# A graph layer on one core: shared scratch for the layer norm, earlier first counts, and h split in four parts

## The chip, the cores and the metric

The kernel runs on one core of one Trainium2 chip, and uses its five engines: TensorE (PE; its weight loads are shown as PEld), VectorE (DVE), ScalarE (ACT), GpSimd (POOL) and SyncE (SP, which only issues transfers). The metric is device time in microseconds (us). A run's time is that of the whole execution; the profile's span is the part in which the program's instructions were recorded.

## The reference

One layer of a graph network with a layer norm ahead of it, over 6,250 nodes with 64 features and 206,250 edges (100,000 random pairs in both directions, and one loop at each node), sorted by target:

```python
h = jnp.maximum(_layernorm(x, axis=-1), 0.0)
msg = h[src] + edge_attr_64
agg = segment_sum(msg, dst, num_segments=6250)
x = x + relu(agg @ W1 + b1) @ W2 + b2
```

The layer norm needs a mean and a variance for each node, and the sums over edges need for each node a sum of rows of h and a sum of edge features.

## The kernel before, in words

**Most of the sum over h goes without a gather.** The first 178 groups of 1,024 edges are put into 1,862 tiles, each of up to 128 edges with targets in V = 3 neighbouring nodes. For a tile, DVE makes 0/1 codes of the edges' sources ("hot", function rows_of_tiles, L832, 18 tiles at a time, from the digits made by encode, L813 and L819, 36 tiles at a time). PE multiplies them to a 128 x 147 table of counts, six tiles to a step (function count, L846, tile pc), and ACT copies the counts into a ring (L852). A block is 84 tiles, 14 steps; there are 22 blocks and 311 steps. While block b is counted, block b - 1 is multiplied with h: 49 products of 128 x 252 accumulate in pv (function products, L864), spread over steps 1 to 8 of the block. For that h is kept as an upper and a lower half side by side (h2; split_upper L547 and L548, split_lower L553). Block 0 has no products beside it.

**The words.** The edges' sources and targets are packed into one word each in DRAM (L579 to L582). To find a tile's words the kernel searches where its first edge lies: a coarse search by DVE and PE, one row of 256 targets per tile fetched by POOL (fetch_row, L283, 15 gathers for 15 groups of 128 tiles), a count by ACT (seek, L298, an activation with an accumulator), and a short sum by DVE (place, L303 and L305). Then POOL gathers the words (fetch_pair), DVE unpacks two groups of tiles at a time (unpack_pair, L655 to L674), and PE and ACT turn them (turn, L688 to L699, with an Exp at L699).

**Edge features.** The features of the edges of these first nodes are loaded in 132 chunks of 1,536 edges straight from DRAM by SP (L405), turned into sums by PE (chunk_sum, L429, with DVE's chunk_hot, L418) into the tile bank, copied out by ACT (take_sums, L437), and placed in pv by PE (chunk_place, L459). The first node of a chunk is found by chunk_starts, chunk_rows, chunk_columns and chunk_index (L324 to L354); fetch_dst gathers the targets, chunk_nodes (L367, L368) and chunk_turn (L375, L376) lay them out.

**The last 24 groups** are gathered: POOL adds rows of h from a table in DRAM to the loaded features, one gather for 128 edges (pfeat, L283, 188 gathers), and PE sums two groups at a time at one of two steps in a block (features_h, L482 to L489, step 5 or 11). The table is written by norm_h (L537 and three transfers at L538); table_rows (L621 to L623) makes the gather's indices.

**"Seconds".** Tiles that have more than 128 edges get a second tile: second_flags, second_ranks and second_words (L721 to L762) find them; each goes from DVE to PE and back to DVE. POOL then gathers their words, they are unpacked over four steps, and turned.

**The order of work is written out by hand.** Every engine runs its instructions in the order of the program. Ahead of step 0 stands a head: loads, searches, packing, mean, centring with squares on ACT, variance, root, scale, table, and the first unpack. Then the loop over steps calls, at each step n, what a dictionary `before` holds for n, then count(n), rows_of_tiles at n % 3 == 1 (for the three steps from n + 2 on), products, and lists of later work. DVE's tiles for three steps are double-buffered, and so is pc. POOL's gathers are issued from a queue by a planner: a clock of HEAD_US for a step of block 0 and STEP_US = 1.4 for a later one, GATHER_US = 2.0 for a gather; features_h of a pair of groups is put at the first step 5 or 11 of a block at which the planner's clock is 4 us past the end of the pair's gathers.

**Scratch.** In the kernel before, the head's scratch (squares, rows of targets, mean, variance, root, and the upper halves) lies in the array of sums, which holds the result of all blocks. So the sums are set to zero late, by ACT in four parts at steps 11 to 14 (L557), and every block's products are added (L895).

## Time and profile before

| what | value |
| --- | --- |
| median of three runs | 504.35 us (502.35 to 505.71) |
| the profiled execution's own time | 503.97 us |
| its span | 502.3 us |
| PE, PEld busy | 429.1 us (85%), 374.7 us (75%) |
| DVE, ACT, POOL busy | 354.3 us (71%), 351.8 us (70%), 374.1 us (74%) |
| mean granted TensorE clock | 0.943 |
| chain that ended last | PE 53%, ACT 14%, DVE 11%, POOL 10%, issue 6%, DMA 5% |

The profile is of one execution. A row of the timeline has the start, the time until the end of the last of the instructions that it merges, the engine, the line, the operation, the tiles written and read, the count, and in brackets the idle time of the engine before it with what ended it. A row of groups has the busy time, the mean in ns, and the idle time before the group. A row of windows has, for a stretch, the busy time and number of instructions of PE, PEld, DVE, ACT and POOL, the granted clock, the share of the DMA engines, and GB/s.

### The profile page before, as it was taken

How to read it: one execution, taken by the hardware profiler on the slowest of the kernel's cores; microseconds unless marked ns; L12 is line 12 of the kernel's file. 1: busy time of each engine (PE TensorE's matmuls, PEld its weight loads, DVE VectorE, ACT ScalarE, POOL GpSimd, SP SyncE). 2: the span in 40 equal slices, each digit the busy share in tenths (PEclk: the TensorE clock that was granted, in tenths of full speed). 3: DMA queues.
4: the chain of work that ended last, by engine and by line, in shares of the span. 5: the costliest groups of instructions: out<-in, count | busy, mean ns of one | idle time of the engine just before them, and what ended most of it. 6: DMA issues, size and time to landing. Idle time of an engine off the chain costs nothing.

```text
span 502.3 us, 17233 instructions
## 1 busy us (share of the span) xinstructions
PE 429.1 (85%) x7194; PEld 374.7 (75%) x7195; DVE 354.3 (71%) x776; ACT 351.8 (70%) x517; POOL 374.1 (74%) x260
## 2 busy tenths in 40 slices
PE   3023799998879998999999999999998999999984
PEld 3023688877768788888788888888887888888864
DVE  4799858977588765787758757787666686677721
ACT  3628978687556767768688778778776677677650
POOL 6866848888887788888888888888888888885000
PEclk9556779999989998999999999999998999999998
DMA  8849637587465665857658758659658568567310
GB/s 225 238 130 301 142 72 190 135 198 174 115 154 127 170 148 133 191 139 187 162 119 211 170 127 217 156 122 246 149 134 216 102 148 204 129 154 168 107 38 15
DMA packets 113355, 78.65 MB, mean 157 GB/s; under 512 B 32736, under 2 KB 108632, under 8 KB 113048
## 3 DMA queue, kind: packets, MB, share of 16 engines
q1 hardware_dynamic: 84356, 65.87, 45.0%
q0 software_dynamic: 28624, 10.11, 17.1%
q10 hardware_dynamic: 292, 1.52, 0.9%
q8 instruction: 58, 0.95, 0.8%
q14 instruction: 25, 0.20, 0.1%
HBM read 73.48 MB, written 3.99 MB: 154 GB/s over the span
## 4 chain that ended last, share of the span: by engine, by line
PE 53%; ACT 14%; DVE 11%; POOL 10%; issue 6%; DMA 5%; DVEq 0%; POOLq 0%; ACTq 0%
PE pv L864 20%; PE pc L846 17%; POOL pfeat L283 9%; ACT ring L852 8%; PE bank L429 6%; DMA pfeat<-table,src_p 4%; DVE hot L832 2%; PE bank L486 2%; PE po L942 2%; ACT kq L695 2%; PE pv L459 2%; PE ph L934 1%; ACT kv L699 1%; DMA firsts_i<-in_dst_g 1%; PE pk L688 1%
## 5 line engine op out<-in xcount | busy, mean ns | idle before, releaser
L283 POOL DMA_INDIRECT pfeat<-table,src_p x188 | 325.9, 1734 | 60.7 <-issue 51.5
L852 ACT ACTIVATE ring<-pc 128x882 fp32r<-128x882 f32 x310 | 276.7, 924 | 82.1 <-PE pc L846 70.4
L846 PE MATMUL pc<-hot 128*128 128x147 fp8e4 x1862 | 178.4, 234 | 25.2 <-ACT ring L852 13.5
L832 DVE TENSOR_TENSOR hot<-at,of 128x576 int32<-128x576 bf16 x208 | 163.2, 826 | 41.4 <-PE pc L846 30.6
L864 PE MATMUL pv<-ring,h 128*128 128x252 f32 (+1 forms) x1078 | 171.3, 296 | 0.8 <-ACT ring L856 0.8
L846 PEld LDWEIGHTS <-hot 128*128 128x128 fp8e4 x1862 | 128.7, 101 | 49.4 <-issue 21.8
L864 PEld LDWEIGHTS pv<-ring,h 128*128 128x128 f32 x1078 | 140.5, 192 | 1.2 <-ACT ring L856 1.0
L429 PE MATMUL bank<-feat,hotf 128*18 128x64 f32 x3168 | 73.5, 225 | 3.1 <-issue 2.0
L429 PEld LDWEIGHTS bank<-feat,hotf 128*18 128x18 f32 x3168 | 49.2, 99 | 21.6 <-issue 4.8
L895 DVE TENSOR_TENSOR sums<-sums,pv 128x252 f32<-128x252 f32 (+4 forms) x34 | 10.0, 323 | 52.8 <-PE pv L864 37.6
L418 DVE TENSOR_TENSOR hotf<-rel,iota 128x432 f32<-128x432 bf16 (+1 forms) x67 | 39.8, 595 | 0.0
L695 ACT ACTIVATE kq<-pk 128x512 bf16<-128x512 f32 (+18 forms) x48 | 18.4, 449 | 12.8 <-PE pk L688 10.2
L813 DVE TENSOR_TENSOR at<-iota_a,kq 128x576 bf16<-128x576 bf16 (+1 forms) x52 | 23.5, 452 | 0.5
L936 ACT ACTIVATE after<-ph,b1s 128x252 f32<-128x252 f32 (+3 forms) x26 | 12.0, 469 | 15.3 <-PE ph L934 14.0
L283 POOL DMA_INDIRECT sums<-in_dst_g,row_i x15 | 17.4, 1162 | 7.0 <-issue 4.3
L819 DVE TENSOR_TENSOR of<-of,kv 128x432 bf16<-128x432 bf16 (+1 forms) x52 | 20.0, 385 | 3.3 <-DVE of L813 0.5
L283 POOL DMA_INDIRECT words<-packed,first_i x15 | 17.7, 1181 | 4.6 <-issue 4.0
L947 DVE TENSOR_TENSOR after<-po,after 126x128 f32<-126x128 f32 (+3 forms) x26 | 7.5, 288 | 18.1 <-PE po L942 18.1
L934 PE MATMUL ph<-sums,w1s 128*128 128x252 f32 (+3 forms) x52 | 17.1, 417 | 3.1 <-issue 1.8
L813 DVE TENSOR_TENSOR of<-iota_w,kq 128x432 bf16<-128x432 bf16 (+1 forms) x52 | 19.5, 374 | 0.0
L324 PE MATMUL pstart<-begins,first 128*1 128x9 f32 (+2 forms) x30 | 1.6, 172 | 17.2 <-DVE sums L509 9.3
L942 PE MATMUL po<-w2s,after 128*126 128x64 f32 (+3 forms) x104 | 15.9, 278 | 0.2 <-issue 0.2
(183 smaller groups left out, 315.6 us busy)
## 6 DMA issues: line engine op xcount, KB each, us to landing
feat<-in_edge SPq DMA_DIRECT2D x132, 384.0 KB
pfeat<-in_edge SPq DMA_DIRECT2D x23, 256.0 KB
pfeat<-table,src_p POOLq DMA_INDIRECT x188
out_y<-after SPq DMA_DIRECT2D x23, 63.0 KB
dstn<-in_dst_g SPq DMA_DIRECT2D x1, 1024.0 KB
table<-xl SPq DMA_DIRECT2D x2, 512.0 KB
after<-in_x SPq DMA_DIRECT2D x4, 252.0 KB
packed<-dstn ACTq DMA_DIRECT2D x1, 768.0 KB
```

The source lines that it names most:

```text
L283: nc.gpsimd.indirect_dma_start(out=rows, out_offset=None, in_=source, in_offset=bass.IndirectOffsetOnAxis(ap=index, axis=0), compute_op=op)
L418: nc.vector.tensor_tensor(hot_of[u][:, :n].rearrange("p c j w -> p (c j) w"), rel[:, c:c + n].rearrange("p c q k -> p (c q k)").unsqueeze( ...
L429: nc.tensor.matmul(bank[q * QP:q * QP + WQ, at:at + D], hot_of[u][:, c, j, :], feats[u][c][:, j, :], start=(k == 0), stop=(k == JP - 1))
L695: nc.scalar.activation(kq[:, q, at:at + n].rearrange("s i k o -> s (i k) o"), pk[:, q, a:a + n].rearrange("s i k -> s (i k)").unsqueeze(2) ...
L813: nc.vector.tensor_tensor(to[:, :n].rearrange("s i k (m o) -> s (i k) m o", o=2), iota_k.rearrange("s (m o) -> s m o", o=2).unsqueeze(1).t ...
L819: nc.vector.tensor_tensor(pairs_of, pairs_of, kv[:, c:c + n].rearrange("s i k o -> s (i k) o").unsqueeze(2) .to_broadcast([P, 2 * n, WE // ...
L832: nc.vector.tensor_tensor(hot[:, :n, c:c + m * A8].rearrange("s i (w a) -> s i w a", a=A8), at[:, o:o + n, k].unsqueeze(2).to_broadcast([P ...
L846: nc.tensor.matmul(pc[:, k, q * K:(q + 1) * K], hot[:, i, :P], hot[:, i, P:P + K], start=True, stop=True)
L852: nc.scalar.activation(to.rearrange("p h (k m) -> p h k m", k=2), pc[:, :, :ST // 2 * K].rearrange("p k (m h) -> p h k m", h=HI), AF.Copy)
L864: nc.tensor.matmul(pvs[b], h2[:, h, :], ring[:, h, c:c + columns_of_block(b)], start=(h == 0), stop=(h == HI - 1))
L934: nc.tensor.matmul(ph[:, :n], w1s, agg[:, start[b]:start[b + 1]], start=True, stop=True)
L942: nc.tensor.matmul(po[:pairs[b], k, :], hid[:, k:2 * pairs[b]:2], w2s, start=True, stop=True)
```

## The change

It makes these edits; the rest of the kernel is as before.

- **Scratch.** A tile "scratch" takes the place of the head's use of the array of sums. It shares its memory with h2, which is made later. Nine rows of targets (ROWS) are kept instead of eleven and four, and row i lies in slot i % 9.
- **Clears.** The sums are cleared in the head: POOL 2,000 columns ahead of its first gather, ACT 1,000 ahead of L562, DVE 2,000 ahead of the packing and the rest (390) behind it. Columns of blocks 0 to 3 (966) are not cleared, and add_products copies into them. ACT's four clears at steps 11 to 14 go.
- **Root.** Square root and reciprocal become Ln and an Exp with scale -0.5, both on ACT; the Newton step on DVE stays. ACT's first activation is an Exp instead of a Sqrt, and an Ln on a column of ones stands behind turn(0).
- **Order of the head.** place covers groups 3 to 6 at once behind the centring; chunk_starts, chunk_rows, chunk_columns and the first unpack follow, then the variance. rows_of_tiles(0) stands ahead of the last third of the variance and of the root. POOL fetches row 0 to 8, words 0 and 1, rows 9 and 10, the targets of chunk group 0 (behind chunk_index), rows 11 to 14, words 2 and 3. ACT seeks rows 9 and 10 ahead of turn(0), and rows 11 to 14 behind it, ahead of the root and of the first ring copy.
- **Into the steps.** norm_scale and the three norm_h with their transfers go to steps 2, 3 and 4, table_rows to step 5, place(7, 4) to step 3 and place(11, 4) to step 5; fetch_h starts at step 5 instead of 2.
- **Split of h.** In four parts (12, 12, 12 and 13 of 49) instead of three, at steps 11 to 18 instead of 7 to 10; the upper halves go through the first 768 or 832 columns of the sums, one after another.
- **Later work.** second_flags, second_ranks, find_groups and second_words go from steps 13, 15, 12, 17 to 18, 20, 21, 22; the unpack of the seconds from 21 to 24 to 26 to 29, and their turn from 25 to 30. take_sums(0) goes from step 14 to 19 and the first chunk_place from 16 to 20.
- **Planner.** HEAD_US is 1.45 instead of 1.7, and POOL's clock opens at step 5 instead of 3.

The core of the diff:

```diff
-HEAD_US = 1.7
+HEAD_US = 1.45
...
-    h2 = consts.tile([P, HI, 2 * D], F32R, name="h2")
+    scratch = consts.tile([P, HI * 2 * D], F32, tag="h2", name="scratch")
...
-    nc.scalar.activation(root, zero, AF.Sqrt)
+    nc.scalar.activation(root, zero, AF.Exp)
...
+    def clear(engine, n):
+        a, z = cleared[0], min(cleared[0] + n, ACOLS)
+        cleared[0] = z
+        if engine is nc.scalar:
+            nc.scalar.activation(agg[:, a:z], zero.to_broadcast([P, z - a]), AF.Copy)
+        else:
+            engine.memset(agg[:, a:z], 0.0)
...
     def norm_root():
         nc.vector.tensor_scalar(var, var, 1.0 / D, EPS, op0=OP.mult, op1=OP.add)
-        nc.scalar.activation(t, var, AF.Sqrt)
+        nc.scalar.activation(tmp, var, AF.Ln)
+        nc.scalar.activation(rs, tmp, AF.Exp, scale=-0.5)
...
+    fourths = [(0, 12), (12, 24), (24, 36), (36, HI)]
...
-            nc.vector.tensor_tensor(to, to, pv[:, c:c + z - a], op=OP.add)
+            if b <= SB:
+                nc.vector.tensor_copy(to, pv[:, c:c + z - a])
+            else:
+                nc.vector.tensor_tensor(to, to, pv[:, c:c + z - a], op=OP.add)
...
-    for i in range(11, IC):
+    for i in range(ROWS, ROWS + 2):
         fetch_row(i)
-    place(6, 3)
+    place(3, 4)
     chunk_starts(0, 2 * RC, "pc", 2)
-    src_hi = late.tile([P, GP * J], I32, tag="part", name="src_hi")
-    table_rows(src_p, src_hi)
-    for f in unpack_pair(0):
-        f()
     chunk_rows(0, 2 * RC)
     load(0)
     chunk_columns(0, 2, "pc", 2)
-    turn(0, P, columns(0))
-    seek(9, 3)
-    norm_scale()
+    nc.vector.tensor_copy(identb, ident)
+    for f in unpack_pair(0):
+        f()
     chunk_index(0, 2)
     fetch_dst(0)
+    for i in range(ROWS + 2, IC):
+        fetch_row(i)
     fetch_pair(2)
-    for k in range(3):
-        norm_h(k)
+    seek(ROWS, 2)
+    turn(0, P, columns(0))
+    nc.scalar.activation(root, ones[:, :1], AF.Ln)
+    seek(ROWS + 2, IC - ROWS - 2)
+    norm_var(0)
+    norm_var(1)
+    rows_of_tiles(0)
+    norm_var(2)
+    norm_root()
     load(1)
...
-        1: [lambda: seek(12, 3), lambda: chunk_nodes(0)],
-        2: [lambda: [fetch_h(g) for g in range(GA, GA + 4)], lambda: chunk_turn(0)],
-        3: [lambda: place(9, 3)],
-        5: [lambda: place(12, 3)],
-        7: [lambda: split_upper(0), lambda: split_upper(1)],
-        8: [lambda: split_lower(0), lambda: split_lower(1)],
-        9: [lambda: split_upper(2)],
-        10: [lambda: split_lower(2)],
-        12: [find_groups],
-        13: [second_flags],
-        15: [second_ranks],
-        17: [second_words],
+        1: [lambda: chunk_nodes(0)],
+        2: [lambda: chunk_turn(0), norm_scale, lambda: norm_h(0)],
+        3: [lambda: norm_h(1), lambda: place(7, 4)],
+        4: [lambda: norm_h(2)],
+        5: [lambda: table_rows(src_p, src_hi), lambda: place(11, 4),
+            lambda: [fetch_h(g) for g in range(GA, GA + 4)]],
+        11: [lambda: split_upper(0)],
+        12: [lambda: split_lower(0)],
...
+        17: [lambda: split_upper(3)],
+        18: [lambda: split_lower(3), second_flags],
+        20: [second_ranks],
+        21: [find_groups],
+        22: [second_words],
...
-    for k in range(4):
-        before.setdefault(11 + k, []).append(lambda k=k: clear(k, 4))
...
-    n = 25
+    n = 30
...
-            at_step(n + STEPS, take_sums, b)
+            at_step(n + STEPS + (0 if b else 5), take_sums, b)
             for u in of_block[b]:
-                at_step(n + STEPS + 2, chunk_place, u)
+                at_step(n + STEPS + (2 if b else 6), chunk_place, u)
...
-            if n == 3:
+            if n == 5:
                 pool[0] = clock(n - 1) + OPENING_US
```

More of the change, by code (lines that the diff above doesn't have):

```diff
@@ L290, in fetch_row @@
     def fetch_row(i):
[L291 to L292 removed]
+        at = rows_at + i % ROWS * L1
+        rows_of[i] = scratch[:, at:at + L1].bitcast(I32)
         gather(rows_of[i], dst_g.rearrange("q h (r k) -> (q h r) k", k=L1), row_i[:, i:i + 1])
@@ L498, in gnn_kernel @@
     xh = xl
-    stat = agg[:, stat_at:stat_at + 4 * HI].rearrange("p (k h) -> p k h", k=4)
-    mean, var, rs, t = (stat[:, k, :] for k in range(4))
+    stat = scratch[:, stat_at:stat_at + 4 * HI].rearrange("p (k h) -> p k h", k=4)
+    mean, var, rs, tmp = (stat[:, k, :] for k in range(4))
     thirds = [(0, 16), (16, 32), (32, HI)]
@@ L514, in norm_center @@
         nc.vector.tensor_tensor(xh[:, h0:h1], xh[:, h0:h1], wide(mean, h0, h1), op=OP.subtract)
-        part = agg[:, squares_at + h0 * D:squares_at + h1 * D].rearrange("p (h d) -> p h d", d=D)
+        part = scratch[:, squares_at + h0 * D:squares_at + h1 * D].rearrange("p (h d) -> p h d", d=D)
         nc.scalar.activation(part, xh[:, h0:h1], AF.Square)
@@ L551, in split_lower @@
     def split_lower(k):
-        h0, h1 = thirds[k]
+        h0, h1 = fourths[k]
         nc.vector.tensor_tensor(h2[:, h0:h1, D:], xh[:, h0:h1], uppers.pop(k), op=OP.subtract)
-    def clear(k, n):
-        a, z = ACOLS * k // n, ACOLS * (k + 1) // n
-        nc.scalar.activation(agg[:, a:z], zero.to_broadcast([P, z - a]), AF.Copy)
-    for i in range(6):
+    clear(nc.gpsimd, 2000)
+    for i in range(ROWS):
         fetch_row(i)
     srcf = src.bitcast(F32)
+    clear(nc.scalar, 1000)
     nc.scalar.activation(srcf, src, AF.Copy)
@@ L586, in gnn_kernel @@
     place(0, 3)
-    for i in range(6, 11):
-        fetch_row(i)
     for k in range(3):
```

43 lines of the change are left out of this document (23 added, 20 removed).

## The prediction

> **What bounds the kernel now.** I read the page's busy shares first, then the stretches of the time, then each stretch's own groups and waits. The stretches: the head from the first full pass over x to the first count, the steps to the seconds, the rest of block 1, and all that follows.
>
> ```profile
> 17.85:42.83 24.98, 3.60 (x26) 2.79 (x27) 23.99 (x52) 12.09 (x30) 17.26 (x14) 0.50 0.64 203
> 42.83:69.90 27.07, 20.56 (x284) 17.62 (x284) 22.07 (x46) 25.80 (x38) 18.20 (x10) 0.70 0.69 170
> 69.90:88.00 18.10, 17.80 (x358) 15.73 (x356) 13.92 (x37) 12.88 (x19) 13.33 (x7) 1.00 0.52 134
> 88.00:480.00 392.00, 367.99 (x6343) 322.29 (x6342) 283.01 (x609) 288.12 (x415) 313.23 (x187) 0.99 0.66 158
> ```
>
> The columns are the stretch, its length, and busy us of PE, PEld, DVE, ACT, POOL, then granted clock, DMA share, GB/s. In the first row DVE works 23.99 of 24.98 us: the head is DVE's. From 69.90 PE works 17.80 of 18.10, and 94% from 88 to 480: what comes early to 69.9 comes early to the end, unless POOL's gathers hold PE. In the second row ACT has 25.80 of 27.07 and DVE 22.07; DVE's missing 5 us are these waits for PE, and the tiles for step 18 (L832, end 69.78) stand behind the first two:
>
> ```profile
> DVE flag L728 <- PE pnext L726: 2.3, 1, 2.3
> DVE fl L744 <- PE prk L736: 1.9, 1, 1.9
> ```
>
> ```profile
> 68.20 1.58 DVE L832 TENSOR_TENSOR hot<-at,of 128x576 int32<-128x576 bf16 x2
> 72.28 0.15 DVE L759 CAST second_i<-pxn 14x1 int32<-14x1 f32 x1 [2.51 <-PE pxn L757]
> ```
>
> So DVE sets the pace from 17.85 to 69.78, with 2.3 + 1.9 us of waiting. A change that only reorders DVE's work can win those 4.2 us, the instructions that it drops or puts behind step 18, and lose the waits that it makes. That is the sum I work out. DVE's prices, by groups from 17 to 70 us (busy us, mean ns, idle):
>
> ```profile
> L832 DVE TENSOR_TENSOR hot<-at,of 128x576 int32<-128x576 bf16 (+1 forms) x14 | 11.0, 827 | 0.3
> L553 DVE TENSOR_TENSOR h<-xl,sums 128x1024 fp32r<-128x1024 f32 (+1 forms) x3 | 3.6, 1239 | 0.0
> L514 DVE TENSOR_TENSOR xl<-xl,sums 128x1024 f32<-128x1024 f32 (+1 forms) x3 | 3.6, 1239 | 0.0
> L537 DVE SCALAR_TENSOR_TENSOR xl<-xl,sums 128x1024 f32<-128x1024 f32 (+1 forms) x3 | 3.6, 1239 | 0.0
> L521 DVE TENSOR_REDUCE sums<-sums 128x16 f32<-128x1024 f32 (+1 forms) x3 | 3.5, 1235 | 0.0
> L509 DVE TENSOR_REDUCE sums<-xl 128x49 f32<-128x3136 f32 x1 | 3.4, 3423 | 2.2 <-issue 2.2
> L547 DVE TENSOR_SCALAR sums<-xl 128x1024 int32<-128x1024 int32 (+1 forms) x3 | 2.0, 701 | 0.0
> L813 DVE TENSOR_TENSOR at<-iota_a,kq 128x576 bf16<-128x576 bf16 x4 | 1.8, 452 | 0.0
> L418 DVE TENSOR_TENSOR hotf<-rel,iota 128x432 f32<-128x432 bf16 x3 | 1.8, 600 | 0.0
> L819 DVE TENSOR_TENSOR of<-of,kv 128x432 bf16<-128x432 bf16 x4 | 1.5, 384 | 0.3
> L813 DVE TENSOR_TENSOR of<-iota_w,kq 128x432 bf16<-128x432 bf16 x4 | 1.5, 377 | 0.0
> ```
>
> A set of tiles (two of L832) is 1.6 us, an encode (L813 twice, L819) 1.2, a chunk_hot (L418) 0.6.
>
> **The change, part by part.** *Clears.* DVE waits 2.2 us ahead of L509, which keeps its place, and I cost the four clears at nothing: DVE's larger one has the wait for the packing in front of it, the small one those 2.2 us; POOL's and ACT's stand ahead of waits for DVE and the loads. Without that cover POOL's would delay the first row by its own length, at most about 2 us. ACT loses four clears from a stretch that it fills; but with the split spread out, DVE and not ACT then sets those steps.
>
> *First counts.* They no longer stand behind norm_h (3.6), the scale (five instructions, about 1.4), the last third of the variance (1.2) and table_rows (0.9): 7.1 us earlier. They get two waits. POOL's rows:
>
> ```profile
> 21.77 1.94 POOL L283 DMA_INDIRECT sums<-in_dst_g,row_i  x1 [0.30 <-issue]
> 24.02 2.03 POOL L283 DMA_INDIRECT sums<-in_dst_g,row_i  x1 [0.30 <-issue]
> ...
> 27.60 0.94 POOL L283 DMA_INDIRECT words<-packed,first_i  x1 [0.30 <-issue]
> ...
> 36.68 1.81 POOL L283 DMA_INDIRECT dstq<-in_dst_g,cols_i  x1 [3.13 <-DVE cols L354]
> ...
> 45.74 1.70 POOL L283 DMA_INDIRECT pfeat<-table,src_p  x1 [3.67 <-DMA table<-xl]
> ```
>
> ```profile
> 30.49 0.29 DVE L655 TENSOR_SCALAR code<-words 128x256 int16<-128x256 int16 x1
> ...
> 34.59 0.44 DVE L529 RECIPROCAL sums<-sums 128x49 f32<-128x49 f32 x1
> ```
>
> The words take the places of the gathers at 21.77 and 24.02, so they are issued by 26.05. Before, those issued by 28.54 were there by 30.49, so landing takes at most 1.95, and I take 28.0. DVE is through centring and chunk starts at about 26.5 (17.85 + 3.4 + 0.2 + 3.6, place, a wait of 0.35 for PE's pstart, chunk rows 0.8): it waits 1.5 us for words. Then unpacking, two thirds of the variance, encode and tiles (3.5 + 0.3 + 2.3 + 1.2 + 1.6) end at 36.9: the first count comes some 5.5 us earlier than 42.83.
>
> *Root.* On DVE the reciprocal (0.44) goes. On ACT root and first ring copy now stand behind the seeks of rows 11 to 14, whose gathers stand on POOL behind the targets' gather, which waits for chunk_index at 31.8. Five gathers with 0.30 between them, by 0.94 each, are issued by 38.0; by 2.03 each, by 43.5. The rows at 21.77 and 24.02 ran beside L514, a DVE operation with two operands, those of 0.94 mostly beside operations with one; the new ones run beside the variance and then encode and tiles. I take two slow ones, 40; landing 1.9 and a seek more, the root is there at about 42.0 (39.9 to 45.5). DVE has finished chunk_nodes and the second set of tiles by 40.9 and waits 1.1 us (0 to 4.6). ACT's table:
>
> ```profile
> 38.54 1.28 ACT L699 ACT_TABLE_LOAD   x1
> ```
>
> This load leaves the path, with the first Exp placed at the start; a new one for Ln fits into ACT's wait for rows. Ln and Exp themselves I price as the root that they replace, twice. The Trainium skill (ScalarE: Activation LUTs, section on table sets) says that one set holds both exp and ln; by that rule nothing stands between the two. Were they in two sets, the load of 1.28 us in the row would come between them and the root 1.3 us later; no run shown so far settles it.
>
> *Norm in the steps.* It is moved work on DVE, not new: scale, three norm_h, table_rows now stand ahead of the tiles for steps 6 and 9, so these come no earlier than before. SP's table transfers follow norm_h at about 46.7 instead of 40; ahead of them on SP are only loads with free buffers. POOL's first gather of the table, 5.7 us behind norm_h before, comes at 52.4 instead of 45.74. Behind it:
>
> ```profile
> POOL words L283 <- DVE second_n L761: 6.0, 1, 6.0
> ```
>
> Those 6.0 us of POOL's waiting shrink to about 1, since second_n, at step 22, finds POOL's queue less far ahead. So the gathers fall some 1.5 us behind the old ones.
>
> ```profile
> 120.36 1.80 POOL L283 DMA_INDIRECT pfeat<-table,src_p  x1 [0.30 <-issue]
> ```
>
> ```profile
> 130.84 1.13 PE L486 MATMUL bank<-after,pfeat 128*64 128x42 f32 x32
> ```
>
> That gather is the last of the second pair of groups; it ends at 122.16, PE uses it at 130.84, at step 61, which keeps its place: 8.7 us, less 1.5, less the landing. Covered. By the planner's constants seven other pairs move by 6 or 8 steps later (33 to 39 up to 299 to 305), the last still ahead of the tail: same work, no price.
>
> *Split.* Four parts cost DVE what three did, 3 x (0.70 + 1.24) = 5.8, but the last, 1.45, now stands behind the tiles for step 18. One scratch for all uppers makes each upper wait for ACT's copy of the one before; with the double buffer of tiles I take 1.1 us of such waits (0 to 2).
>
> *Ledger at the tiles of step 18:* 69.78, less 4.2 (waits), 0.44 (reciprocal), 1.3 (the short instructions of groups, flags and ranks, my estimate), 1.45 (last part), plus 1.5, 0.35, 1.1, 1.1 (waits made) = 66.3. The last part of the split and the flags with PE's pnext (1.45 + 1.3) follow ahead of the count of step 18: 69.1.
>
> ```profile
> 70.65 0.83 PE pxn L755 x30
> 71.48 0.76 PE pxn L757 x30
> ...
> 73.49 0.40 PE pc L846 x6
> ```
>
> Before, that count came at 73.49: a lead of 4.4 us.
>
> *Seconds.* Of PE's work that stood ahead of it, pxn (0.83 + 0.76), the ranks' prk and the first chunk_place (about 0.55 each) now follow: 2.7 us back. And at step 22 DVE waits for pxn and then has an encode, a set of tiles and a chunk_hot to make (1.2 + 1.6 + 0.6), while PE has two counts and some six products, about 1.7: a stall of 0 to 2. I take 1.0. The lead left is 0.7 us, between 4.5 ahead (no wait for the root, none for the split, no stall) and 5 behind (root at 45.5, all waits full).
>
> **The sum.** 503.97, the profiled execution's own time, less 0.7: 503.3 us. That execution lies 0.4 under the median of three. About 1% is what a measurement of this kernel can tell from no change.
>
> **The rivals.** *The lead of the first count is kept.* If the waits for words and root are short and the seconds fall into gaps, 5.5 us arrive at the end: 498.5. For it speaks PE's 17.80 of 18.10 behind step 16, against it DVE's full head: tiles past the second set wait for moved work.
>
> *Seconds in the loaded steps make it slower.* Before, DVE waited 2.3, 1.9 and 2.5 us for PE in three round trips, two of them while PE had little to do. Now each stands in block 1's products. If each also stops PE for its length, 6.7 us are lost against a lead of 1.7: 503.97 - 1.7 + 6.7 = 509.0. It decides against the change from 1.7 us of stalls on, and by over 1% from 6.7. Against it: DVE makes tiles three steps ahead, 3 to 4 us of PE's work.
>
> *The words land no sooner.* Then the unpack starts at 30.49 again, 2.5 us later than I take: 505.8. For it: the rows show the packed words stored by 26.35, not yet by 21.8; against it, their store on ACT stands behind L579, which ends 2.2 us ahead of L509.
>
> *POOL is locked out by DVE.* All five gathers by 2.03: the root 3.5 us later, 506.8. The Trainium skill (SBUF — State Buffer, section on who interferes with whom) says that a DVE instruction with two SBUF inputs contends with a GpSimd instruction that reads SBUF, while a reduction doesn't; by that rule the encode and tiles would hold the later rows' gathers. The rows of 1.94 and 2.03 against 0.94 agree.
>
> **How the numbers follow.** My forecast has 0.46; words late 0.09 and POOL locked 0.11, which both lie within 1% of before; the kept lead 0.2, the slower seconds 0.14. Faster by over 1%: 0.2; within 1%: 0.66; slower: 0.14. The likeliest case's own range is 499.5 to 506. For 8 in 10 I take in the kept lead and leave out most of the slowest: 498.5 to 507.5.
>
> **What would show it.** The first count (L846) near 37, ACT's first ring copy near 42, with rows 11 to 14 as its releaser; DVE idle ahead of L655 and ahead of the scale; tiles for step 18 near 66; POOL's first pfeat near 52 with a shorter wait for second_n; PE idle at steps 22 to 24. The prediction is wrong if the ring copies start before 40, if PE shows no gap behind pxn, or if L486 at step 61 waits for a gather.

## The result, and the profile after

The changed kernel took 509.25 us in the median of four executions (507.89 to 512.88), the kernel before 503.35 (500.67 to 505.71): ratio 1.015, 95% interval 1.0102 to 1.0198. The forecast was 503.3 with a range up to 507.5. The rival of the seconds in the loaded steps had said 509.0. The profiled execution took 507.89 us, with a span of 506.2. Ratios and intervals here and below are taken from fast executions (none over 1.5% above the fastest of its kernel), medians from all, so a ratio need not be that of the medians (here 1.012).

The stretches of the profile after, cut at the same work as before (to the first count, to the seconds, to step 30, and the 392 us that follow), with the same columns:

```profile
17.80:37.34 19.54, 3.63 (x27) 2.55 (x27) 16.57 (x37) 11.57 (x28) 12.84 (x11) 0.50 0.80 252
37.34:69.83 32.49, 19.99 (x277) 16.50 (x277) 27.68 (x52) 23.64 (x40) 18.52 (x12) 0.75 0.53 145
69.83:91.90 22.07, 20.00 (x358) 17.79 (x358) 13.54 (x40) 11.92 (x16) 13.72 (x9) 0.85 0.45 108
91.90:483.90 392.00, 366.72 (x6346) 321.23 (x6346) 283.97 (x614) 288.87 (x417) 311.12 (x188) 0.99 0.66 159
```

The head is 5.4 us shorter, the steps behind it 5.4 longer. The loss stands in the third row: 22.07 us instead of 18.10, with PE busy for 20.00 instead of 17.80 on the same 358 matmuls. PE's work became slower there: the granted clock is 0.85 and was 1.00.

The head first, by three engines' instructions in order of time (start, length, then in brackets the idle time ahead and its releaser). DVE:

```profile
28.80 0.29 DVE L661 TENSOR_SCALAR code<-words 128x256 int16<-128x256 int16 x1 [2.14 <-DMA words<-packed,first_i]
...
34.70 0.38 DVE L819 TENSOR_TENSOR of<-iota_w,kq 128x432 bf16<-128x432 bf16 x1
...
35.70 1.58 DVE L838 TENSOR_TENSOR hot<-at,of 128x576 int32<-128x576 bf16 x2
...
42.77 0.21 DVE L542 TENSOR_TENSOR scratch<-scratch 128x49 f32<-128x49 f32 x1 [1.52 <-ACT scratch L538]
...
66.55 1.57 DVE L838 TENSOR_TENSOR hot<-at,of 128x576 int32<-128x576 bf16 x2
68.04 0.58 DVE L560 TENSOR_SCALAR sums<-xl 128x832 int32<-128x832 int32 x1
68.66 1.02 DVE L566 TENSOR_TENSOR h<-xl,sums 128x832 fp32r<-128x832 f32 x1
69.61 0.17 DVE L729 TENSOR_SCALAR ends<-first 128x15 f32<-128x15 f32 x1
```

ACT, around the root:

```profile
38.33 0.51 ACT L310 ACTIVATE scratch<-scratch,nhalf 128x256 bf16<-128x256 int32 x1 [1.57 <-DMA scratch<-in_dst_g,row_i]
...
40.96 0.23 ACT L537 ACTIVATE scratch<-scratch 128x49 f32<-128x49 f32 x1
41.20 1.28 ACT L538 ACT_TABLE_LOAD   x1
42.49 0.24 ACT L538 ACTIVATE scratch<-scratch 128x49 f32<-128x49 f32 x1
```

POOL, the gathers of rows 11 to 14, the first of the table, and the one behind second_n:

```profile
33.39 0.95 POOL L295 DMA_INDIRECT scratch<-in_dst_g,row_i  x1 [0.30 <-issue]
34.64 0.95 POOL L295 DMA_INDIRECT scratch<-in_dst_g,row_i  x1 [0.30 <-issue]
35.89 1.38 POOL L295 DMA_INDIRECT scratch<-in_dst_g,row_i  x1 [0.30 <-issue]
37.58 0.95 POOL L295 DMA_INDIRECT scratch<-in_dst_g,row_i  x1 [0.30 <-issue]
...
51.94 2.17 POOL L295 DMA_INDIRECT pfeat<-table,src_p  x1 [10.69 <-DVE first_i L317]
...
80.78 1.28 POOL L295 DMA_INDIRECT words<-packed,second_i  x1 [6.22 <-DVE second_n L767]
```

The head went much as forecast: the words at 28.80, the root's chain at 42.77, tiles for step 18 done at 68.12, the first gather of the table at 51.94. Step 18 came 3.0 us earlier than before. PE's first count, and then what it met from step 18 on:

```profile
37.34 1.66 PE L852 MATMUL pc<-hot 128*128 128x147 fp8e4 x12 [4.44 <-DVE hot L838]
...
69.83 0.40 PE L731 MATMUL pnext<-ends,shift 128*128 128x15 f32 x2 [2.27 <-DVE ends L729]
...
70.65 1.73 PE L870 MATMUL pv<-ring,h 128*128 128x252 f32 x7
...
77.29 1.07 PE L870 MATMUL pv<-ring,h 128*128 128x252 f32 x7
...
83.89 0.53 PE L441 MATMUL bank<-feat,hotf 128*18 128x64 f32 x24 [1.95 <-DVE hotf L430]
...
97.60 0.58 PE L387 MATMUL pdst<-shift,dstq 128*128 128x128 f32 x3 [2.31 <-DVE dstq L380]
```

Three times PE waits about 2 us for DVE. Behind the first wait seven products take 1.73 us; a few steps on, seven take 1.07. The same place cut into stretches, the three waits and what follows each:

```profile
67.50:69.83 2.33, 0.07 (x1) 0.00 (x0) 2.25 (x5) 1.17 (x2) 2.02 (x2) 1.00 0.32 27
69.83:74.38 4.55, 4.54 (x30) 4.42 (x31) 2.41 (x7) 2.65 (x4) 3.94 (x3) 0.62 0.25 54
74.38:81.90 7.52, 7.52 (x180) 6.86 (x178) 2.38 (x11) 2.84 (x4) 1.30 (x2) 1.00 0.44 108
81.90:83.89 1.99, 0.04 (x2) 0.01 (x1) 1.99 (x4) 0.91 (x1) 1.68 (x2) 1.00 0.09 21
83.89:88.11 4.22, 4.22 (x90) 3.36 (x90) 4.08 (x14) 2.08 (x3) 3.60 (x3) 0.60 0.49 114
88.11:95.25 7.14, 7.03 (x111) 6.21 (x103) 4.34 (x12) 6.06 (x11) 5.93 (x4) 1.00 0.79 186
95.25:97.60 2.35, 0.05 (x1) 0.03 (x1) 2.28 (x7) 0.43 (x1) 2.05 (x2) 1.00 0.17 14
97.60:102.09 4.49, 4.49 (x28) 4.26 (x28) 4.28 (x12) 2.23 (x3) 3.58 (x4) 0.62 0.17 15
```

Each wait of 2.0 to 2.35 us is followed by 4.2 to 4.55 us of full work at a mean granted clock of 0.60 to 0.62. That costs another 4.4 x 0.39 = 1.7 us each time. The Trainium skill (TensorE: Matmul & The Clock Gate, section on oscillation) warns of idle gaps above some 3.4 us; here gaps of 2 us were enough, and the measurement decides.

Such a wait does not always have the low clock behind it. In another profile of this kernel (after_third, below) PE waits at the same three places for 2.28, 1.95 and 1.68 us, and the clock falls behind the second alone (0.60 from 82.45 to 86.67). Behind the first and the third it stays full:

```profile
69.96:74.51 4.55, 4.55 (x57) 4.39 (x57) 3.30 (x11) 3.31 (x5) 3.94 (x3) 1.00 0.27 55
...
95.47:99.96 4.49, 4.49 (x65) 4.20 (x65) 4.28 (x12) 2.77 (x4) 3.77 (x3) 1.00 0.17 15
```

PE does 57 and 65 matmuls there, where the profile above has 30 and 28 in as many us. What decides whether the clock falls, no run shows. What DVE waited for in these steps, in the first profile after:

```profile
DVE second_i L765 <- PE pxn L763: 4.5, 1, 4.5
DVE code L661 <- PE pc L852: 2.6, 1, 2.6
...
DVE fl L750 <- PE prk L742: 2.0, 1, 2.0
...
DVE flag L734 <- PE pnext L732: 0.7, 1, 0.7
```

The chain reads like this. The last part of the split and ends (68.04 to 69.78) hold up pnext, and PE idles. DVE then waits for pxn 4.5 us, and at 80.33 it has an encode, tiles and a hotf to make: PE idles again until 83.89. At step 31 DVE waits 2.6 us: the unpacking of the next pair needs the single code buffer, which the seconds' turn, at step 30, has only just read (by the kernel's text; e6 below tries it). DVE comes late to dstq of step 33, and PE idles a third time.

The starts of ACT's ring copies (L852 before, L858 after; one each step, in us) show where the time goes over the whole kernel:

| step | 0 | 18 | 28 | 42 | 84 | 168 | 210 | 294 | last |
|---|---|---|---|---|---|---|---|---|---|
| before | 43.8 | 73.9 | 85.9 | 105.9 | 168.8 | 290.4 | 347.2 | 462.8 | 483.9 |
| after | 42.6 | 70.9 | 89.9 | 114.7 | 176.0 | 296.2 | 351.4 | 466.9 | 487.8 |

A lead of 3.0 us at step 18, 4.0 behind at step 28, 8.8 behind at step 42, 3.9 behind at the end. The loss of 11.8 us stands in 24 steps. What comes back behind step 42 differs from execution to execution (373 to 380 us from step 42 to the last, over the profiles of before, after and the first eight experiments), so below I read the steps to 42 from profiles and the whole from medians.

### The profile page after: what moved, and what is told of

It reads as the page before. It is cut to its first block, busy times and chain, and to the rows that moved or that the text cites. A ratio compares the mean times of both kernels' runs of the same rounds, so it can differ in the third digit from the quotient of the medians.

```text
span 506.2 us, 17236 instructions
## 1 busy us (share of the span) xinstructions
PE 430.0 (85%) x7194; PEld 374.6 (74%) x7195; DVE 354.7 (70%) x777; ACT 349.9 (69%) x518; POOL 370.1 (73%) x261
## 3 DMA queue, kind: packets, MB, share of 16 engines
q10 hardware_dynamic: 292, 1.52, 0.9%
## 4 chain that ended last, share of the span: by engine, by line
PE 65%; DVE 12%; ACT 12%; issue 6%; POOL 2%; DMA 2%; DVEq 0%; ACTq 0%; POOLq 0%
PE pv L870 24%; PE pc L852 21%; PE bank L441 9%; ACT ring L858 7%; DVE hot L838 4%; PE bank L498 3%; PE ph L945 2%; POOL scratch L295 2%; PE pv L471 2%; ACT kq L701 2%; PE po L953 2%; ACT kv L705 1%; DMA scratch<-in_dst_g,row_i 1%; PE pk L694 1%; DMA firsts_i<-in_dst_g 1%
## 5 line engine op out<-in xcount | busy, mean ns | idle before, releaser
L295 POOL DMA_INDIRECT pfeat<-table,src_p x188 | 320.9, 1707 | 67.7 <-issue 51.2
L858 ACT ACTIVATE ring<-pc 128x882 fp32r<-128x882 f32 x310 | 276.0, 922 | 86.7 <-PE pc L852 74.5
L852 PE MATMUL pc<-hot 128*128 128x147 fp8e4 x1862 | 178.8, 234 | 25.5 <-ACT ring L858 11.1
L838 DVE TENSOR_TENSOR hot<-at,of 128x576 int32<-128x576 bf16 x208 | 163.2, 825 | 43.8 <-PE pc L852 27.8
L852 PEld LDWEIGHTS <-hot 128*128 128x128 fp8e4 x1862 | 128.6, 101 | 50.0 <-issue 19.5
L906 DVE TENSOR_TENSOR sums<-sums,pv 128x252 f32<-128x252 f32 (+3 forms) x28 | 8.2, 322 | 43.5 <-PE pv L870 39.4
L819 DVE TENSOR_TENSOR at<-iota_a,kq 128x576 bf16<-128x576 bf16 (+1 forms) x52 | 23.5, 452 | 1.0 <-ACT kq L701 0.4
L295 POOL DMA_INDIRECT scratch<-in_dst_g,row_i x15 | 16.0, 1066 | 5.3 <-issue 4.3
L819 DVE TENSOR_TENSOR of<-iota_w,kq 128x432 bf16<-128x432 bf16 (+1 forms) x52 | 19.4, 373 | 0.0
L295 POOL DMA_INDIRECT dstq<-in_dst_g,cols_i x5 | 6.2, 1248 | 15.8 <-PE pdst L387 7.5
```

The source lines that it names most:

```text
L295: nc.gpsimd.indirect_dma_start(out=rows, out_offset=None, in_=source, in_offset=bass.IndirectOffsetOnAxis(ap=index, axis=0), compute_op=op)
L819: nc.vector.tensor_tensor(to[:, :n].rearrange("s i k (m o) -> s (i k) m o", o=2), iota_k.rearrange("s (m o) -> s m o", o=2).unsqueeze(1).t ...
L838: nc.vector.tensor_tensor(hot[:, :n, c:c + m * A8].rearrange("s i (w a) -> s i w a", a=A8), at[:, o:o + n, k].unsqueeze(2).to_broadcast([P ...
L852: nc.tensor.matmul(pc[:, k, q * K:(q + 1) * K], hot[:, i, :P], hot[:, i, P:P + K], start=True, stop=True)
L858: nc.scalar.activation(to.rearrange("p h (k m) -> p h k m", k=2), pc[:, :, :ST // 2 * K].rearrange("p k (m h) -> p h k m", h=HI), AF.Copy)
```

## Experiments

Three theories at the start. A: the seconds in block 1's products cost the time. B: the late root does. C: the planner's moved groups of features do. The runs come in five groups, each with its own runs of before, whose medians were 503.67, 502.94, 497.28, 497.52 and 497.92 us. The first two groups ran on two chips near 503, where before also stood in the result (503.35); the third ran on a chip near 497, and the last two on one other chip near 497. The changed kernel itself was run again in the third and fourth group only, so in the first two its 1.015 is that of the result.

**Seconds early (e1), root early (e2), seconds late in the kernel before (e3), old steps of the features (e4).**

```
e1    12: [lambda: split_lower(0), find_groups],   13: [lambda: split_upper(1), second_flags],
      15: [lambda: split_upper(2), second_ranks],  17: [lambda: split_upper(3), second_words],
      n = 25                                       (changed kernel: 21, 18, 20, 22 and n = 30)
e2  - seek(ROWS + 2, IC - ROWS - 2)
    + 1: [lambda: seek(ROWS + 2, IC - ROWS - 2), lambda: chunk_nodes(0)],
e3    before, with 18: [second_flags], 20: [second_ranks], 21: [find_groups], 22: [second_words], n = 30
e4    HEAD_US = 1.7,  pool[0] = clock(n - 3) + OPENING_US
```

> The changed kernel with find_groups, flags, ranks and words of the seconds back at steps 12, 13, 15 and 17, and their unpacking and turn at steps 21 and 25. If the seconds in block 1's products cost the time (theory A), the waits of PE, DVE and POOL behind steps 18 to 32 go, 7 to 9 us come back, but the three waits for PE (2.3, 2.0 and some 1 us) stand ahead of the tiles for step 18 again and eat most of the lead of 3: 502 to 505 us, a ratio to before of 0.998 to 1.004. If the late root is what costs (theory B), or the shifted groups of features (theory C), the time stays at 508 to 511, ratio 1.011 to 1.018.

> The changed kernel with the seeks of rows 11 to 14 behind the first ring copy, at step 1, so that ACT's Ln and Exp no longer stand behind them. Theory B (late root): root some 2.3 us earlier (near 40.4 instead of 42.73), and most of it reaches the end: 506.5 to 507.5, ratio 1.009. Theory A (seconds): the tiles for step 18 come 1 to 2 us earlier, but the waits behind them grow by as much: 508.5 to 510, ratio 1.013 to 1.016. Theory C: no change, 509.3.

> The kernel before with one part of the change alone: flags, ranks, groups and words of the seconds at steps 18, 20, 21 and 22, unpacking and turn at 26 and 30. Theory A: DVE's 2.3 and 1.9 us of waiting ahead of step 18 are won, and the same losses as in the changed kernel (some 12 us between steps 18 and 42, some of it regained) follow: 507 to 511 us, ratio 1.008 to 1.016. Theories B and C, in which the seconds are not the cause: 500 to 503.5, ratio 0.993 to 1.000.

> The changed kernel with the planner's constants set so that the twelve groups of features stand at the steps of before (33, 61, 89, 117, 137 and so on to 299) instead of 39, 61, 95, ... 305. Theory C (the shifted groups, the last of them six steps ahead of the end): 504 to 506 us, ratio 1.002 to 1.006. Theories A and B: within 1 us of the changed kernel, 508.5 to 510.5, ratio 1.013 to 1.017; PE may also wait for the first pair of groups, whose gathers end at 93.9 us with step 33 at 98.9.

| kernel | median us | ratio to before | interval |
|---|---|---|---|
| e1 | 504.85 | 1.0001 | 0.9963 to 1.0039 |
| e2 | 509.81 | 1.0065 | 1.0015 to 1.0116 |
| e3 | 509.69 | 1.0093 | 1.0065 to 1.0121 |
| e4 | 509.67 | 1.0114 | 1.0071 to 1.0157 |

e1 and e3 bear A out from both sides: moving the seconds alone takes the loss out of the changed kernel, and puts most of it into the old one. In the profiles e1 reaches step 42 at 105.8 us, as before does; e3 at 115.0, as the changed kernel does. e2's root came at 40.5, 2.2 us earlier, yet step 28 at 89.6 and not at 89.9: the lead was gone. Its time alone does not shut B out: 1.0065 lies nearer to the 1.009 that B forecast than to A's 1.013 to 1.016, and its profile reaches step 42 at 111.0, 3.7 us ahead of the changed kernel's. But between steps 28 and 42 PE waits for dstq nearly as long as there (2.00 us), and only the clock behind it differs (1.00 from 96.99 to 101.48), as it does between two profiles of one kernel. That e1, with its root as late, shows no loss speaks against B as the main cause. e4 is within the changed kernel's interval: C is not the loss either, on this chip.

**Which part of the seconds (e5, e6), root early besides (e7), seconds in stages (e9).** e5 has e1's steps but n = 30. e6 lets the next pair's unpacking start a step later. e7 is e1 and e2 together. e9 is e7 with each round trip cut into an asking and a fetching step.

```
e6  unpack_later(n - (3 if i == 2 else 4), lambda i=i: unpack_pair(i))
e9  6: [second_ends],  8: [second_next],  10: [second_flags],  12: [..., second_prk, find_groups],
    14: [..., second_ranks],  15: [..., second_pxn],  17: [..., second_words],   n = 25
```

> The changed kernel with groups, flags, ranks and words of the seconds back at steps 12, 13, 15 and 17, but their unpacking and turn left at steps 26 and 30. It parts theory A in two. A1, the three round trips between DVE and PE inside block 1's products cost the time: about as with all of the seconds early, ratio to before 0.999 to 1.004 (503 to 506). A2, the cost is the unpacking at 26 to 30, whose code buffer is still held when the next pair is unpacked at step 31 (DVE waited 2.63 us there): half or more of the loss stays, ratio 1.006 to 1.012.

> The changed kernel with the unpacking of the pair of lists that follows the seconds at steps 32 to 35 instead of 31 to 34, so that it finds the code buffer free or nearly so. A2: DVE's 2.63 us wait at step 31 and PE's 2.3 us wait for dstq at step 33 go, ratio 1.006 to 1.010 (507 to 508.5). A1: at most 1 us of it reaches the end, ratio 1.012 to 1.017 (509 to 511).

> The changed kernel with both edits: seconds at 12 to 17, 21 and 25, and the seeks of rows 11 to 14 behind the first ring copy. If DVE's pace to step 18 carries the root's delay to the end, the root near 40.4 brings 1.5 to 2.5 us: 500.5 to 502.5, ratio 0.993 to 0.998. If the steps to 18 are bound by something else, no change against the seconds alone: ratio 0.999 to 1.002.

> The same two edits, but the seconds cut at each round trip: ends at step 6, PE's pnext at 8, flag at 10, PE's prk at 12, ranks and pick at 14, PE's pxn at 15, second_i and second_n at 17, so that DVE comes to each result steps after PE was asked for it. A1 says that the waits for PE are what the seconds cost wherever they stand: DVE's waits for pnext, prk and pxn (0.7, 2.0 and some 1 to 4 us) all but vanish, the tiles for step 18 come 2 to 4 us earlier, 498.5 to 501, ratio 0.989 to 0.995. If DVE's waiting was idle time that the steps have anyway: ratio 0.997 to 1.001.

| kernel | median us | ratio to before | interval |
|---|---|---|---|
| e5 | 507.22 | 1.0104 | 1.0055 to 1.0153 |
| e6 | 509.48 | 1.0120 | 1.0083 to 1.0158 |
| e7 | 504.68 | 0.9990 | 0.9945 to 1.0034 |
| e9 | 506.17 | 1.0066 | 1.0032 to 1.0101 |

The two halves stand apart in the profiles. Steps 18 to 28 and 28 to 42, the kernel before:

```profile
73.90:85.90 12.00, 11.87 (x243) 10.11 (x243) 10.40 (x28) 9.10 (x14) 10.64 (x5) 1.00 0.60 148
85.90:105.90 20.00, 18.89 (x341) 16.79 (x341) 18.09 (x42) 15.00 (x24) 17.05 (x10) 1.00 0.71 177
```

The changed kernel:

```profile
70.90:89.90 19.00, 16.94 (x327) 14.90 (x327) 12.11 (x36) 9.40 (x11) 11.26 (x7) 0.82 0.44 105
89.90:114.70 24.80, 20.36 (x338) 17.86 (x336) 17.71 (x44) 15.41 (x27) 20.84 (x14) 0.93 0.58 133
```

e5, with the chain early and the unpacking late:

```profile
72.30:86.20 13.90, 12.58 (x250) 10.57 (x250) 10.32 (x26) 8.99 (x12) 12.07 (x7) 1.00 0.55 137
86.20:110.00 23.80, 20.00 (x339) 17.66 (x338) 18.85 (x44) 15.65 (x27) 20.14 (x13) 0.93 0.56 133
```

e6, with the chain late and the code buffer free:

```profile
70.90:89.80 18.90, 16.84 (x327) 14.76 (x326) 12.13 (x36) 9.42 (x11) 11.26 (x7) 0.82 0.45 107
89.80:109.50 19.70, 18.45 (x338) 16.16 (x337) 17.43 (x44) 15.51 (x27) 16.65 (x11) 1.00 0.61 145
```

e5 mends the first row and not the second (19.00 to 13.90; 24.80 to 23.80), e6 the second and not the first (24.80 to 19.70, clock 0.93 to 1.00). So in the profiles both A1 and A2 hold, each for its own steps. In the times less than these 5 us came back: neither interval shuts out the changed kernel's 1.015. e9's expectation failed: at 1.0066 it was no better than e7. Its profile reaches step 12 at 63.0, e7's at 59.8. The asking at step 8 met ACT's last reading of the turn of step 7, which holds the same bank of PSUM (PE's first product for pnext waited 1.81 us for it), and DVE stood waiting in the steps that it paces:

```profile
57.04 0.18 DVE L742 SCALAR_TENSOR_TENSOR flag<-pnext,ends 128x15 bf16<-128x15 f32 x1 [4.71 <-PE pnext L736]
```

**The changed kernel as yardstick, the late chain without its round trips (e10), early chain with late unpacking and the pair shifted (e12), e7 again.** e10 keeps PE's work at its late place, and asks two or three steps before it fetches.

```
e10   15: [..., second_ends], 16: [..., second_next], 19: [second_flags, second_prk],
      22: [second_ranks, second_pxn], 24: [second_words];  unpacking 28 to 31, turn at 31;  e6's shift
e12   e5 with e6's shift
```

> The changed kernel as it is, as the yardstick of this chip for the other three. All theories: ratio to before 1.011 to 1.018.

> The changed kernel with the seconds as late as it has them (PE's prk at step 19, pxn at 22, turn at 31), but each result fetched by DVE two or three steps after PE was asked for it (ends 15, pnext 16, flag 19, ranks 22, second_n 24), and the next pair unpacked at 32 to 35. PE does the same work at the same place; only the round trips are gone. If the waits cost (A1), steps 18 to 28 fall from 19.0 to 14 or 15 us (11.9 of before and 2.7 of moved work) and steps 28 to 42 to about 20: ratio 1.000 to 1.006. If PE's moved work in full steps and the lower clock cost: steps 18 to 28 stay at 17 to 19, ratio 1.007 to 1.012.

> The changed kernel with groups, flags, ranks and words early (12 to 17), unpacking and turn late (26 and 30), and the next pair unpacked a step later (32 to 35). With the pair at its old place this kernel stood at 1.0104. If the code buffer is what the late unpacking costs (A2), steps 28 to 42 fall from 23.7 to about 20 us and the ratio to 0.998 to 1.004. If it is DVE's added work between 26 and 34 as such, it stays at 1.006 to 1.012.

> The kernel with seconds early and rows 11 to 14 off the root once more, in more rounds: in its profile it reached step 42 at 103.6 us, 2.3 ahead of before and 2.2 ahead of the one with the seconds alone, and yet the median showed nothing. If a lead at step 42 reaches the end: ratio 0.993 to 0.997. If later steps take it back (gathers of the table, which start 6 us later than before): 0.999 to 1.003.

| kernel | median us | ratio to before | interval |
|---|---|---|---|
| after_again | 497.86 | 1.0001 | 0.9971 to 1.0030 |
| e10 | 495.00 | 0.9948 | 0.9918 to 0.9978 |
| e12 | 490.34 | 0.9845 | 0.9791 to 0.9899 |
| e7_again | 489.04 | 0.9817 | 0.9773 to 0.9862 |

On this chip the changed kernel was as fast as before, against every expectation. The distances to the changed kernel held: e7 is 1.8% under it here, and was 1.6% under it by the ratios on the first chips. e12 is 1.6% under it, where e5, which lacks the shift, was 0.5% under it on another chip, and its steps 28 to 42 took 20.1 us. So freeing the buffer removes what late unpacking costs. e10 is 0.5% under it. e10, steps 18 to 28 and 28 to 42:

```profile
70.40:83.50 13.10, 12.86 (x305) 11.09 (x303) 8.29 (x23) 9.09 (x13) 9.54 (x6) 1.00 0.58 142
83.50:109.90 26.40, 20.82 (x338) 18.22 (x338) 21.07 (x56) 15.84 (x28) 22.44 (x14) 0.87 0.52 116
```

In the first row PE does most of the moved work (305 matmuls; before had 243, the changed kernel 327) in 13.10 us at full clock. That work is some 1 us (12.86 against before's 11.87 busy); the other 6 of the changed kernel's 19.00 were the waits and the low clock behind them. The second row shows a new wait: the words, asked for at step 24, were late at step 28.

```profile
85.44 0.21 DVE L661 TENSOR_SCALAR code<-words 14x128 int16<-14x128 int16 x1 [4.13 <-DMA words<-packed,second_i]
```

**Before and after on one chip, with e1 and e7 beside them.**

> The kernel before, unchanged, for a profile of it on the same chip as the changed kernel's. If the two kernels differ only ahead of step 42 (theory A), its stages behind step 84 have the same lengths here as those of the changed kernel. If something in the later steps weighs on the one and not on the other, depending on the chip (theory D: short stalls of PE for its instructions, on some chips 2 us in 42 steps, on others 0.8), they differ by several us. Ratio 0.998 to 1.002.

> The changed kernel, unchanged. It stood at 1.015 on one chip and 1.000 on another. Theory A with the chip as a second factor: 1.012 to 1.017 if PE's stages from step 126 to 168 take 57 us here, 0.997 to 1.003 if they take 55.5.

> The changed kernel with all of the seconds early. Relative to the changed kernel in this call: 0.984 to 0.988 (theory A, the loss of steps 18 to 42 is the seconds, on any chip), or nearer to 1 than 0.993 if the chip decides whether the seconds cost.

> The same with rows 11 to 14 off the root. Relative to the kernel with the seconds early alone in this call: 0.995 to 0.997 if the root's 2 us reach the end, 0.999 to 1.001 if they don't.

| kernel | median us | ratio to before | interval |
|---|---|---|---|
| before_copy | 497.05 | 1.0005 | 0.9967 to 1.0043 |
| after_third | 498.20 | 0.9999 | 0.9971 to 1.0027 |
| e1_again | 490.81 | 0.9859 | 0.9816 to 0.9902 |
| e7_third | 488.96 | 0.9860 | 0.9786 to 0.9935 |

The seconds cost the same here as on the first chips: e1_again is 1.4% under the changed kernel, where e1 was 1.5% under it. The profile of after_third shows less of it, 38.2 us in steps 18 to 42 against before_copy's 31.2; of its three waits only one had the low clock behind it, and its execution, of 495.02 us, was the shortest of ten. The root's 2 us stay inside the intervals; whether they reach the end is not settled. The changed kernel's ratio went with PE's pace, as expected: its steps 126 to 168 took 55.5 us here and 57.5 on the chip of the result. What the two kernels do behind step 42 differs too. Before's ring copies on this chip, and those of the changed kernel:

| step | 0 | 18 | 28 | 42 | 84 | 168 | 210 | 294 | last |
|---|---|---|---|---|---|---|---|---|---|
| before_copy | 43.5 | 74.4 | 86.4 | 105.6 | 165.8 | 281.7 | 339.4 | 450.4 | 476.3 |
| after_third | 42.8 | 71.0 | 88.2 | 109.2 | 169.3 | 287.3 | 341.1 | 453.8 | 475.0 |

The changed kernel is 5.6 us behind at step 168 and 1.3 ahead at the end. It gains 3.9 us in steps 168 to 210, loses 1.7 in the next 84, and gains 4.7 in the last sixteen. In both stretches of gain before_copy's PE waits for gathers of the table:

```profile
335.72 0.31 PE L486 MATMUL bank<-after,pfeat 128*64 128x42 f32 x2 [1.58 <-DMA pfeat<-table,src_p]
...
461.64 0.31 PE L486 MATMUL bank<-after,pfeat 128*64 128x42 f32 x2 [2.47 <-DMA pfeat<-table,src_p]
```

The granted clock behind them is 0.62 (336.03 to 340.50) and 0.68 (461.64 to 466.20). These are the groups at steps 207 and 299, which the change moves to 215 and 305. On the chip of the first profile the last gather was issued as late, but PE came 12 us later. The first profile of before, POOL's last gather:

```profile
458.46 1.88 POOL L283 DMA_INDIRECT pfeat<-table,src_p  x1 [0.31 <-issue]
```

and its use on PE there:

```profile
470.22 0.90 PE L486 MATMUL bank<-after,pfeat 128*64 128x42 f32 x24
```

In before_copy POOL's last gather starts almost as late:

```profile
456.73 2.08 POOL L283 DMA_INDIRECT pfeat<-table,src_p  x1 [0.30 <-issue]
```

PE had come to that group at 457.85. POOL's pace is the same in both profiles: 188 gathers, the first at 45.74 and 45.05. PE's is not. Where PE's steps run shorter, the gathers bind.

**The features' steps alone (e13), and taken from the changed kernel (e4 again).**

```
e13   before, with one line changed:   OPENING_US = 14.0      (was 8.0)
```

> The kernel before with the planner's opening time at 14.0 instead of 8.0, by which the twelve groups of features stand at the steps of the changed kernel (39, 61, 95, 117, 145, 165, 187, 215, 235, 263, 285, 305), and nothing else. On a chip whose median of before is near 497: if the gathers of the table are what holds before there (theory D; PE's waits of 1.6 us at step 207 and 2.5 us at step 299 in the profile of before_copy), 4 to 6 us go, ratio 0.987 to 0.993. On a chip whose median is near 503, where no such wait stands in the profile: 0.997 to 1.002 in either case. If the seconds' place explains all by itself (theory A alone): 0.997 to 1.002 on any chip.

> The changed kernel with the old steps of the features, once more. On a chip near 497: theory D takes from it what the changed kernel won there, ratio to before 1.006 to 1.013 instead of 1.000. On a chip near 503: 1.011 to 1.017, as the changed kernel itself. Theory A alone: the changed kernel's own ratio of that chip, 1.000 near 497.

| kernel | median us | ratio to before | interval |
|---|---|---|---|
| e13 | 491.21 | 0.9877 | 0.9849 to 0.9904 |
| e4_again | 506.00 | 1.0172 | 1.0143 to 1.0201 |

One constant makes before 1.2% faster on this chip, and the last group no longer waits:

```profile
465.14 0.90 PE L486 MATMUL bank<-after,pfeat 128*64 128x42 f32 x24
```

Its steps 168 to 210 take 53.8 us instead of 57.8, the 84 behind them 113.2 instead of 111.0 (the group of step 207, 1.1 us of PE's work, now lies in them), and steps 294 to the last 21.2 instead of 25.9: of the two waits the last was worth the most. e4_again is not settled. Its ratio, 1.0172, goes with five of its seven executions (504.87 to 507.09); the two shortest, 496.64 and 502.94 us, stand at 0.998 and 1.010 of before. The only profiled one is that of 496.64 us, and it shows no long wait for gathers. So no trace shows why the five are long, and they lie above the 1.006 to 1.013 that theory D (gathers of the table hold PE) forecast.

So three of four corners are settled on the chips near 497. Early seconds with the old steps of the features (before) stand at 1.000; early seconds with the new steps at 0.988 (e13) and 0.986 (e1_again); late seconds with the new steps (the changed kernel) at 1.000; late seconds with the old steps (e4_again) are open. The changed kernel with early seconds, 0.986, is not measurably better than before with the new steps, 0.988; the intervals overlap. So the rest of the change, all that the forecast's ledger was made of, is worth less than these runs can tell. Several versions beat both kernels on those chips: e1, e12, e7 (0.982 and 0.986), and before with one constant (0.988); on the first chips e1 and e7 stood at 1.000 and 0.999. On the chips near 503 the new steps show no gain in the changed kernel (e4 at 1.0114, the changed kernel at 1.015), and the seconds' 1.5% stand alone; e13 was not run there.

## Why the prediction was wrong

*The head: right.* Forecast and measured: words 28.0 and 28.80; first count 36.9 and 37.34; root 42.0 and 42.73; DVE's wait for it 1.1 and 1.52; waits for words 1.5 and 2.14; tiles for step 18 66.3 and 68.12; count of step 18 69.1 and 70.30; first gather of the table 52.4 and 51.94. The lead at the count of step 18 was 4.4 by the forecast, 3.2 as measured, and 3.0 at the ring copy. Two slips are in the working: the ledger's terms add up to 66.4 and not 66.3, and a first count at 36.9 is 5.9 us ahead of 42.83, not 5.5 (measured: 5.5). The ledger also lacked a wait of 1.6 us that DVE had for PE's turn (ahead of the tiles at 56.66); the waits of the split were 0.7 instead of 1.1.

*The root: right by luck.* I took two slow gathers and no table load, and the sum to 42.0 left out the last seek, Ln and Exp that it names (together some 1.1 us in the trace). The gathers of rows 11 to 14 took 0.95, 0.95, 1.38 and 0.95, so at most one was held up, and the last ended at 38.53 instead of 40. The one at 34.64 ran beside L819 and the one of 1.38 beside L838, both DVE operations with two inputs (the first gather started ahead of its L819, the second behind the start of L838); the rule of the Trainium skill (SBUF — State Buffer, section on who interferes with whom) shows in the second alone. In return a load of 1.28 us stood between Ln and Exp, where the Trainium skill (ScalarE: Activation LUTs, section on table sets) names one set for both. The measurement decides: the forecast's 1.3 us for two sets was the term to take.

*The step that failed: the seconds.* The forecast took "1.0 us" for the stall, and 2.7 us of moved work. Between steps 18 and 42 the first profile after lost 11.8 us: three PE waits of 2.3, 2.0 and 2.3 us (the first just ahead of step 18's copy), 1.7 us behind each at the lower clock, and the moved work, some 1 us in e10. Two waits inside the 24 steps, 4.3, three times 1.7 and the 1 are 10.4 of the 11.8; the rest is not assigned. The forecast priced a wait at its length; in this execution it cost nearly twice that. Where the clock fell behind one wait alone (after_third), 7.0 us were lost. The forecast saw the round trips (the rival at 509.0) and put them down at 0.14, because DVE makes its tiles three steps ahead. At step 18 that cover was gone: PE waited for ends at 69.83 since the forecast's own ledger had put the last split part and ends ahead of it.

*The unpacking: not seen.* The forecast had no term for the seconds' move to steps 26 to 30 beside the next pair's unpacking at 31. One code buffer made it 4 to 5 us (e6: steps 28 to 42 from 24.80 to 19.70).

*POOL's wait for second_n: wrong.* Said to shrink from 6.0 to 1 us; it was 6.22, since second_n came 8 us later (second_i 72.28 before, 80.33 after) and POOL's queue, from its first gather of the table on, was late too. The gathers behind it had room: PE waited for none in these steps.

*Seven groups of features at other steps, "same work, no price": right on the chips near 503, wrong on those near 497*, where in the kernel before it is worth 1.2% (e13), about what the seconds lose. The forecast's ratio of 0.999 is met there (1.000), by luck.

*The rivals.* The kept lead failed; words late and POOL locked out did not happen; the slower seconds came true to 0.3 us, though by another sum: two of its three waits were not the ones priced, and the clock did the rest.

*Open.* Why PE's steps run longer on some chips: the changed kernel's PE idles 4.6 of 112.7 us in steps 126 to 210 on the first, 1.7 of 109.4 on another, partly in short waits put down to issue; no run tried that, and whether it is the chip or something else that differs between the groups isn't shown. Why the clock falls behind some waits of 2 us and not behind others. Why e5 and e6 gave back only 0.5 and 0.3% in their times, some 2 us, where each profile shows 5 us at step 42, while both edits together (e12) gave 1.6%. Each of these profiles is one execution: three of the changed kernel took 43.8, 41.9 and 38.2 us for steps 18 to 42.

## What to carry to other kernels

Count a stall of PE in full steps at its length, and allow for a stretch of low clock behind it, which here cost 1.7 us behind all three waits of some 2 us in one execution and behind one of three in another. When a chain of round trips is moved, list what stands ahead of each request on the asking engine, and which single buffer its last consumer holds. A queue with a fixed pace, like POOL's gathers, may have room on one chip and bind on another, so an edit that moves its due times has a price even where the work is the same.

## What the runs showed of the hardware

PE idle for 2.0 to 2.35 us came back at a mean granted clock of 0.60 to 0.62 for 4.2 to 4.55 us in the first profile after, three times of three; in after_third, behind 2.28, 1.95 and 1.68 us, one time of three (0.60; the others 1.00). Seven products of 128x252 took 1.73 us at the low clock and 1.07 at the full one. ACT loaded a table for 1.28 us between Ln and Exp. The kernel before stood near 503 us on two chips and near 497 on two others, with POOL's last gather at 458.46 and 456.73 us, and the ratio of the two kernels was 1.015 on one and 1.000 on others.
